# Routing the last tile by column halves, on rows that are not yet normalized

## The chip, the cores and the metric

The kernel runs on one core of one Trainium2 chip. The metric is the device time of one execution in microseconds (us): the median of several executions, 684.8 us for the kernel before. Below, PE or TensorE is the matrix engine, DVE or VectorE the vector engine, ACT or ScalarE the engine for activations, POOL or GpSimd the general engine, and SP the queue that issues the large loads. Each engine works through its own queue in order, and waits for others by semaphores.

## The reference, cut to what matters

One layer of a perceiver: cross-attention to a context of 1601 rows, a linear-attention block with an MLP, and a mixture of experts. There are 8 x 64 = 512 tokens of width 512. What the change touches is the end of the MLP, the layer norm after it and the routing:

```python
# end of the second block: x is (512, 512)
x = x + (gelu(h2 @ w1 + b1) @ w2 + b2) + ...
m = layernorm(x)                        # (x - mean) / sqrt(var + 1e-5)
router_logits = m @ w_router            # (512, 8)
top_w, top_i = jax.lax.top_k(router_logits, 2)
top_w = softmax(top_w)
for e in range(8):
    hmid = silu(m @ w0[e]) * (m @ w1[e])
    out = out + gating[:, e:e+1] * (hmid @ wo[e])
return x + out
```

## The kernel before, in words

All data are float32. The 512 tokens are four tiles (NT = 4) of 128 tokens, tokens on partitions; a row of 512 columns is KC = 4 chunks of 128. The order of the instructions on every engine is the order in which the program writes them out by hand. PSUM has eight banks: four in rotation for short products (`mm_bank`) and four for accumulators (`acc_bank`).

The MLP has 16 chunks of hidden columns. The first eight are multiplied by w2 for all four tiles at once; the last eight (HELD) are kept in SBUF and multiplied tile by tile (`last_chunks`), so that the routing of one tile can run beside the products of the next. `finish(t)` (lines 826 to 840) adds tile t's product to the residual row `xs`, takes its mean and variance with `bn_stats`, normalizes it into `mn`, and sends `mn` to a scratch in DRAM (`mn_dram`, on ACT's queue) and `xs` to the output (on GpSimd's). Then, while TensorE works on the chunks of tile t + 1:

- `turn_m` (L851, L853) transposes the four chunks of `mn` and ACT copies them to SBUF.
- `route` (L859 to L874) multiplies them by the router's columns, and DVE picks the two largest of the eight logits, their places, and marks them (`hot`, `member`).
- `rank_tile` (L888 to L894) counts by two small products how many earlier tokens have chosen each expert, and compares the rank with the numbers 1 to 128 (`slot`): a one-hot matrix for expert 0.
- `first_rows` (L899) multiplies `mn` by this one-hot: this gathers the first 128 rows of expert 0, already transposed, in one PSUM bank over all four tiles. These are called the gathering products.
- `tabulate` (L913 to L928) works out where each token stands in a table in DRAM and writes it with two indirect DMAs of GpSimd, each of which waits for the one before; `count_tile` keeps the running counts.

For the last tile there is no next tile; `turn_m`, `route`, `rank_tile` and `first_rows` follow each other. ACT copies the gathered rows (`xgT_first`, L959), DVE does the last two `tabulate`, a product sums the counts (L966), DVE copies them out (`count`, L968), and works out the gates (L971 to L981), which ACT writes to `mn_dram` (L982).

Then the experts run one after the other. `whole_tile` makes for each expert four products with the upper weights (`up`, L1081), silu and product (`gated`, L1044, L1046), transposes (`hidden_t`, L1052) and the lower product (`y`, L1089). The rows of the other experts are gathered from `mn_dram` by indirect DMAs (`fetch`, L1017), whose places come from the table (`late`, L984 and L1007 to L1011). The experts' weights pass through a ring of 12 tiles in SBUF, 1 MB each, that the SP queue refills (L192) as they are used up. The expert stage opens its own pool over the same eight PSUM banks, and its banks are placed in the order in which they are first named.

Of the kernel before, what the change touches and what calls it, by code (L numbers as in the profile page):

```python
# [20 lines left out]
P = 128  # L21
# [25 lines left out]
def perceiver_kernel(  # L47
# [189 lines left out]
    for e in range(NE):  # L237
# [18 lines left out]
        slot, pattern=[[1, P]], base=1, channel_multiplier=0, allow_small_or_imprecise_dtypes=True  # L256
    )
# [278 lines left out]

    for g in range(4):
        key_group(0, g)
    for g in range(2):
        key_group(1, g)  # L540
    for t in range(NT):
# [15 lines left out]
        if t == NT - 3:  # L557
            late_loads()

# [265 lines left out]

    def finish(t):
# [4 lines left out]
        mv = small.tile([P, 2], F32, tag="mv1", name=f"mv_m_{t}")  # L831
        nc.vector.bn_aggr(mv, st)
        rstd = small.tile([P, 1], F32, tag="rstd1", name=f"rstd_m_{t}")
        nc.scalar.activation(rstd, mv[:, 1:2], AF.Sqrt, bias=eps)
        nc.vector.reciprocal(rstd, rstd)
        nc.vector.tensor_scalar(
            mn[:, t, :D], xs[:, t, :], mv[:, 0:1], rstd, ALU.subtract, ALU.mult
        )
        nc.scalar.dma_start(mn_dram[t * P : (t + 1) * P, :D], mn[:, t, :D])
# [6 lines left out]
    m_ts = {}  # L846

    def turn_m(t):
        bank = mm_bank(f"tr_m_{t}")
        for c in range(KC):  # L850
            nc.tensor.transpose(bank[:, c * P : (c + 1) * P], mn[:, t, c * P : (c + 1) * P], ident)  # L851
        m_ts[t] = mlp2.tile([P, KC, P], F32, tag="mT", name=f"m_t_{t}")
        nc.scalar.copy(m_ts[t].rearrange("p c q -> p (c q)"), bank)  # L853

    def route(t):

        bank = mm_bank(f"router_{t}")
        for c in range(KC):
            nc.tensor.matmul(  # L859
                bank[:, :NE], m_ts[t][:, c, :], router[:, c, :], start=(c == 0), stop=(c == KC - 1)  # L860
            )
        logits = small.tile([P, NE], F32, tag="logits", name=f"logits_{t}")
        nc.vector.tensor_copy(logits, bank[:, :NE])
        nc.vector.max(out=top[:, t, :], in_=logits)
        where = small.tile([P, NE], mybir.dt.uint32, tag="where", name=f"where_{t}")
        nc.vector.max_index(out=where, in_max=top[:, t, :], in_values=logits)
        nc.vector.tensor_copy(chosen[:, t, :], where[:, :2])
# [3 lines left out]
            chosen[:, t, :, None].to_broadcast([P, 2, NE]),  # L871
# [4 lines left out]
    def count_tile(t):  # L876
        if t == 0:
            nc.vector.tensor_copy(members[:, 0, :], member[:, 0, :])
        else:
            nc.vector.tensor_tensor(members[:, t, :], members[:, t - 1, :], member[:, t, :], ALU.add)  # L880

    onehots = {}

    def rank_tile(t):

        bank = mm_bank(f"rank_{t}")
        if t > 0:
            nc.tensor.matmul(bank[:, :NE], ones, members[:, t - 1, :], start=True, stop=False)  # L888
        nc.tensor.matmul(bank[:, :NE], earlier, member[:, t, :], start=(t == 0), stop=True)
        nc.vector.scalar_tensor_tensor(  # L890
            rank[:, t, :], bank[:, :NE], 1.0, member[:, t, :], ALU.add, ALU.mult
        )
        onehots[t] = mlp2.tile([P, P], F32, tag="onehot", name=f"onehot_{t}")
        nc.vector.tensor_scalar(onehots[t], slot[:, :P], rank[:, t, 0:1], None, ALU.is_equal)  # L894

    def first_rows(t):

        for c in range(KC):
# [4 lines left out]
                start=(t == 0 and c == 0),  # L903
                stop=(t == NT - 1),
                skip_group_check=True,
            )

# [32 lines left out]
    for t in range(1, NT):  # L940

        last_chunks(t, range(0, 4))
        turn_m(t - 1)
        last_chunks(t, range(4, 5))
        route(t - 1)
        last_chunks(t, range(5, 7))
        rank_tile(t - 1)
        last_chunks(t, range(7, HELD))
        finish(t)
        first_rows(t - 1)  # L950
        if t > 1:
            tabulate(t - 2)
        count_tile(t - 1)
    turn_m(NT - 1)
    route(NT - 1)
    rank_tile(NT - 1)
    first_rows(NT - 1)
    xg_t0 = moe.tile([P, KC, P], F32, name="xgT_first")
    nc.scalar.copy(xg_t0.rearrange("p c q -> p (c q)"), first_bank)  # L959
# [452 lines left out]
```

## Time and profile before

| what | us |
|---|---|
| median of 3 runs | 684.8 (684.72 to 687.41) |
| the profiled execution's own time | 685.44 |
| its span | 683.7 |
| mean granted clock of TensorE | 0.983 of full speed |
| TensorE busy | 638.9 (93% of the span) |
| VectorE busy | 179.1 (26%) |
| ScalarE busy | 128.2 (19%) |
| GpSimd busy | 61.7 (9%) |

The span is counted from the first to the last event of one execution; the time of that execution has 1.7 us around it. Times in the text are from the start of the span. In the profile, PE stands for TensorE's products and PEld for its loading of weights; an entry such as `[2.01 <-DVE mn L836]` says that the engine stood idle for 2.01 us and that DVE's instruction of line 836 ended that. A float32 product over 512 columns appears as two records. The granted clock is 1.00 at full speed and 0.50 at half.

### The profile page before, as it was taken

What the parts mean: (1) busy time and instruction counts of PE and PEld (TensorE: products, weight loads), DVE (VectorE), ACT (ScalarE), POOL (GpSimd) and SP (SyncE); (2) the same over time, 40 slices, a digit from 0 to 9 for tenths busy, and PEclk for the clock granted to TensorE, in tenths of its full rate; (3) what the DMA queues carried; (4) which work ended last, traced back from release to release, by engine and by line L of the source; (5) the groups of instructions that cost most, each with busy time, mean ns of one, the idle gap of its engine ahead of it and who ended that gap; (6) DMA issues with size and microseconds to landing.
All of it is one profiled execution on the core that took longest, in us unless ns stands there. A gap on an engine that the chain in (4) does not pass through costs nothing. (4 is left out here: it accounts for less than half of the span.)

```text
span 683.7 us, 6217 instructions
## 1 busy us (share of the span) xinstructions
PE 638.9 (93%) x2376; PEld 296.2 (43%) x2376; DVE 179.1 (26%) x403; ACT 128.2 (19%) x240; POOL 61.7 (9%) x81
## 2 busy tenths in 40 slices
PE   4998989799999999999999998898999999989993
PEld 3643434244444444445444455543444344434441
DVE  4011323132228687670000035310311101110100
ACT  2241223220132121122011200211111111111110
POOL 2000000000000000041000002331012202120000
PEclk9999999999999999999999999699999999999998
DMA  8999999999601103021311323127397595694711
GB/s 328 418 420 385 418 385 413 370 367 422 232 13 62 62 0 124 1 69 55 112 62 73 106 79 126 61 61 265 136 390 257 199 357 175 233 348 175 283 17 18
DMA packets 24222, 138.04 MB, mean 202 GB/s; under 512 B 4164, under 2 KB 4164, under 8 KB 11896
## 3 DMA queue, kind: packets, MB, share of 16 engines
q1 hardware_dynamic: 20056, 129.90, 49.0%
q0 software_dynamic: 3024, 6.58, 4.3%
q10 hardware_dynamic: 1104, 1.07, 0.4%
q8 instruction: 23, 0.38, 0.2%
q14 instruction: 15, 0.12, 0.1%
HBM read 132.56 MB, written 4.97 MB: 201 GB/s over the span
## 5 line engine op out<-in xcount | busy, mean ns | idle before, releaser
L1081 PE MATMUL up<-e_up,xgT 128*128 128x512 f32 x224 | 100.2, 595 | 1.2 <-PEq L1310 1.2
L1081 PEld LDWEIGHTS up<-e_up,xgT 128*128 128x128 f32 x224 | 40.9, 190 | 50.4 <-issue 50.4
L1089 PE MATMUL y<-e_wo,hidT 128*128 128x512 f32 x128 | 61.0, 599 | 0.0
L792 PE MATMUL mlp<-w,hid_sb 128*128 128x512 f32 x128 | 58.8, 597 | 0.0
L1046 DVE TENSOR_TENSOR mid<-up,act 128x256 f32<-128x256 f32 x35 | 14.9, 425 | 164.2 <-ACT act L1044 159.7
L771 PE MATMUL hid<-v_sb,w 128*128 128x512 f32 (+2 forms) x144 | 56.6, 545 | 0.0
L472 PE MATMUL av<-ctx,eT 128*64 128x512 f32 x192 | 48.4, 617 | 7.3 <-DMA ctx<-in_ctx_dram 6.5
L423 PE MATMUL sc<-ctxT,pw_t 128*64 128x401 f32 (+1 forms) x256 | 48.1, 501 | 0.7 <-DMA ctxT<-in_ctx_T_dram 0.7
L771 PEld LDWEIGHTS hid<-v_sb,w 128*128 128x128 f32 x144 | 26.2, 190 | 29.1 <-issue 27.3
L792 PEld LDWEIGHTS mlp<-w,hid_sb 128*128 128x128 f32 x128 | 23.4, 190 | 24.9 <-issue 24.9
L1044 ACT ACTIVATE act<-up 128x256 f32<-128x256 f32 x35 | 13.4, 383 | 104.5 <-PE up L1081 95.7
L786 POOL TENSOR_TENSOR xin<-xin,b_bc 128x512 f32<-128x512 f32 x4 | 5.1, 1263 | 295.3 <-DVE rstd_h L728 291.1
L423 PEld LDWEIGHTS sc<-ctxT,pw_t 128*64 128x64 f32 x256 | 20.3, 136 | 26.3 <-issue 22.9
L1062 POOL DMA_INDIRECT out_dram<-y_sb,dst_late x11 | 16.8, 1529 | 161.1 <-ACTq L1310 103.7
L1089 PEld LDWEIGHTS y<-e_wo,hidT 128*128 128x128 f32 x128 | 22.4, 190 | 19.5 <-issue 19.1
L595 PE MATMUL wk<-h_t,wk 128*128 128x512 f32 x64 | 29.5, 604 | 0.0
L595 PE MATMUL wq<-h_t,wq 128*128 128x512 f32 x64 | 29.4, 602 | 0.0
L532 PE MATMUL v<-wv,h_t 128*128 128x512 f32 x64 | 28.7, 597 | 0.6 <-DVE h_t L519 0.6
L472 PEld LDWEIGHTS av<-ctx,eT 128*64 128x64 f32 x192 | 13.9, 140 | 35.3 <-issue 24.6
L691 PE MATMUL wo<-wo,a_t 128*128 128x512 f32 x64 | 28.6, 597 | 0.0
L671 DVE RECIPROCAL rden<-rden 128x512 f32<-128x512 f32 x8 | 26.8, 3354 | 0.3
L828 DVE TENSOR_TENSOR xs<-mlp,xs 128x512 f32<-128x512 f32 x4 | 2.8, 692 | 87.3 <-PE mlp L792 87.3
(230 smaller groups left out, 653.1 us busy)
## 6 DMA issues: line engine op xcount, KB each, us to landing
e_up<-in_L_ffn_up_dram SPq DMA_DIRECT2D x32, 1024.0 KB, 7.9
ctx<-in_ctx_dram SPq DMA_DIRECT2D x24, 1024.0 KB, 17.4
ctxT<-in_ctx_T_dram SPq DMA_DIRECT2D x24, 802.0 KB, 15.7
e_wo<-in_L_ffn_wo_dram SPq DMA_DIRECT2D x16, 1024.0 KB, 10.0
w<-in_L_attn_w_dram SPq DMA_DIRECT2D x8, 1024.0 KB, 11.7
ctxT<-in_ctx_T_dram SPq DMA_DIRECT2D x8, 796.0 KB, 16.7
big_up<-in_L_ffn_up_dram SPq DMA_DIRECT2D x4, 1024.0 KB, 7.9
wv<-in_L_attn_wv_dram SPq DMA_DIRECT2D x2, 1024.0 KB, 13.0
```

The source lines that it names most:

```text
L423: nc.tensor.matmul(sc[h * S : (h + 1) * S, :width], pw_t[:, c, (2 * t + h) * S : (2 * t + h + 1) * S], keys[h][:, c, :], start=(c == 0), s ...
L472: nc.tensor.matmul(av[h * S : (h + 1) * S, :], e_t[:, 4 * g + j, h * S : (h + 1) * S], rows[h][:, j, :], start=(g == 0 and j == 0), stop=F ...
L532: nc.tensor.matmul(bank, h_t[:, c, t * P : (t + 1) * P], wv_n[:, c, :], start=(c == 0), stop=(c == KC - 1))
L595: nc.tensor.matmul(bank, w[:, c, (j % 4) * P : (j % 4 + 1) * P], h_t[:, c, :], start=(c == 0), stop=(c == KC - 1),)
L671: nc.vector.reciprocal(rden, rden)
L691: nc.tensor.matmul(wo_banks[t], a_t[:, j, t * P : (t + 1) * P], wo_r[j // 4][:, j % 4, :], start=(j == 0), stop=(j == nj - 1),)
L771: nc.tensor.matmul(hid_banks[f][:, tokens], w[:, c, (f % 4) * P : (f % 4 + 1) * P], h2_t[:, c, tokens], start=(c == 0), stop=(c == KC - 1),)
L792: nc.tensor.matmul(acc[t], hid[:, t * P : (t + 1) * P], need("w2", f // 4)[:, f % 4, :], start=(f == 0), stop=(f == FF // P - 1),)
L1046: nc.vector.tensor_tensor(hid, bank[:, FQ:], act, ALU.mult)
L1062: nc.gpsimd.indirect_dma_start(out=out, out_offset=bass.IndirectOffsetOnAxis(ap=dst[:n, :], axis=0), in_=y_sb[:n, :], in_offset=None, boun ...
L1081: nc.tensor.matmul(bank, xg_t[:, c, :], up_of[q][:, c, :], start=(c == 0), stop=(c == KC - 1))
L1089: nc.tensor.matmul(y, h_t[:, j, :], w[:, 2 * (q % 2) + j, :], start=(q + j == 0), stop=(q + j == NQ))
```

## The change

The change rewrites the routing, above all that of the last tile.

- The router is centred: `centre_router`, called once in the attention stage, takes from each router column its mean over the 512 rows (`router_c`). The logits of rows that are not normalized then differ from those of normalized rows only by a factor for each row (one over the standard deviation), which does not change the order. So `turn_m` transposes `xs` in place of `mn`, and the difference of the two largest logits is multiplied by the factor (`rstds`) before the softmax.
- DVE reads the logits straight from PSUM, and the places of the two largest without a cast; two copies leave the chain. The one-hot is made from the rank's product directly, with `slot0` (0 to 127) and `member`.
- The last eight chunks of the last tile are multiplied by column halves: columns 0 to 255 first, then 256 to 511 into a bank of their own (`second_bank`). The first half is added, transposed and taken through the router while TensorE multiplies the second.
- The rows of the last tile are normalized by ACT, and no longer by DVE.
- The gathering products of tiles 0 to 2 leave the loop; they stand between the steps of the last tile's routing, four, two, five and one at a time, and those of tile 3 follow.
- The gathered rows are copied in two halves, by ACT and by DVE; `tabulate` for tiles 2 and 3 stands behind them on DVE. `tabulate` for tiles 0 and 1 comes one tile earlier. The sum of counts lies in a bank of the accumulators, and the expert stage names some of its banks first, so that they are placed elsewhere.

The core of the diff:

```diff
+    def centre_router():
+        bank = mm_bank("router_sums")
+        for c in range(KC):
+            nc.tensor.matmul(bank[:, :NE], ones, router[:, c, :], start=(c == 0), stop=(c == KC - 1))
+        nc.vector.scalar_tensor_tensor(
+            router_c, bank[:, None, :NE].to_broadcast([P, KC, NE]), -1.0 / D, router, ALU.mult, ALU.add,
+        )
...
             late_loads()
+            centre_router()
...
-    def turn_m(t):
+    def turn_m(t, chunks=range(KC)):
...
-            nc.tensor.transpose(bank[:, c * P : (c + 1) * P], mn[:, t, c * P : (c + 1) * P], ident)
+            nc.tensor.transpose(bank[:, i * P : (i + 1) * P], xs[:, t, c * P : (c + 1) * P], ident)
...
-        logits = small.tile([P, NE], F32, tag="logits", name=f"logits_{t}")
-        nc.vector.tensor_copy(logits, bank[:, :NE])
+        logits = route_banks[t][:, :NE]
         nc.vector.max(out=top[:, t, :], in_=logits)
...
-        nc.vector.tensor_scalar(onehots[t], slot[:, :P], rank[:, t, 0:1], None, ALU.is_equal)
+        nc.vector.tensor_scalar(
+            onehots[t], slot0, bank[:, 0:1], member[:, t, 0:1], ALU.is_equal, ALU.mult
+        )
...
+    st = small.tile([P, 2, 6], F32, tag="st2", name="st_m_last")
+    half_chunks(0, range(0, 5))
+    turn_m(t - 1)
+    rank_before(t - 1)
+    half_chunks(0, range(5, HELD))
+    for h in range(2):
+        nc.vector.tensor_tensor(xs[:, t, halves[h]], acc[t][:, halves[h]], xs[:, t, halves[h]], ALU.add)
+    logits_of(t - 1)
+    choose(t - 1)
+    half_chunks(1, range(0, 3))
+    turn_m(t, range(0, 2))
+    nc.vector.bn_stats(st[:, 0, :], xs[:, t, halves[0]])
+    half_chunks(1, range(3, 5))
+    rank_tile(t - 1)
+    count_tile(t - 1)
+    half_chunks(1, range(5, 7))
+    logits_of(t, range(0, 2))
+    rank_before(t)
+    half_chunks(1, range(7, HELD))
+    nc.vector.tensor_tensor(xs[:, t, halves[1]], second_bank[:, :HD], xs[:, t, halves[1]], ALU.add)
+    first_rows(4)
+    turn_m(t, range(2, KC))
+    nc.vector.bn_stats(st[:, 1, :], xs[:, t, halves[1]])
+    mv, rstd = moments(t, st)
+    nc.vector.scalar_tensor_tensor(neg_mean, mv[:, 0:1], -1.0, rstd, ALU.mult, ALU.mult)
+    nc.scalar.activation(mn[:, t, :D], xs[:, t, :], AF.Identity, bias=neg_mean, scale=rstd)
+    first_rows(2)
+    logits_of(t, range(2, KC))
+    choose(t)
+    first_rows(5)
+    rank_tile(t)
+    first_rows(1)
+    count_tile(t)
+    first_rows(KC)
+
+    bank = acc_bank("counts")
+    nc.tensor.matmul(bank[:, :NE], ones, members[:, NT - 1, :], start=True, stop=True)
+    xg_t0 = [moe.tile([P, 2, P], F32, name=f"xgT_first_{h}") for h in range(2)]
+    for h, copy in enumerate([nc.scalar.copy, nc.vector.tensor_copy]):
+        copy(xg_t0[h].rearrange("p c q -> p (c q)"), first_bank[:, halves[h]])
+    write(NT - 1)
     for t in range(NT - 2, NT):
         tabulate(t)
-
-    bank = mm_bank("counts")
-    nc.tensor.matmul(bank[:, :NE], ones, members[:, NT - 1, :], start=True, stop=True)
     count = moe.tile([P, NE], F32, name="count")
     nc.vector.tensor_copy(count, bank[:, :NE])
...
     nc.vector.tensor_tensor(e2, top[:, :, 1], top[:, :, 0], ALU.subtract)
+    nc.vector.tensor_tensor(e2, e2, rstds, ALU.mult)
...
+        for tag, n in (("mm1", 2), ("y1", 1), ("yw", 1)):
+            pse.tile([P, 512], F32, tag=tag, bufs=n, name=f"place_{tag}")
```

## The prediction

> **What bounds the kernel now.** I read the page first, then the timeline around the step between the MLP and the experts, then busy time by stretches cut to the steps of the clock, then what GpSimd waits for. The page:
>
> ```profile
> span 683.7 us, 6217 instructions
> PE 638.9 (93%) x2376; PEld 296.2 (43%) x2376; DVE 179.1 (26%) x403; ACT 128.2 (19%) x240; POOL 61.7 (9%) x81
> ...
> PE   4998989799999999999999998898999999989993
> ...
> PEclk9999999999999999999999999699999999999998
> ```
>
> TensorE is busy 93% of the span, so time comes only from its few holes. The clock row has one low slice, the 26th (427 to 444 us), inside what the change touches: the end of the MLP and the routing of the last tile. The timeline there:
>
> ```profile
> 424.15 1.05 PE L899 MATMUL first_rows<-onehot,mn 128*128 128x128 f32 x8
> ...
> 424.42 0.69 DVE L828 TENSOR_TENSOR xs<-mlp,xs 128x512 f32<-128x512 f32 x1 [0.54 <-PE mlp L792]
> ...
> 427.22 0.66 PE L851 MATMUL tr_m<-ident,mn 128*128 128x128 f32 x4 [2.01 <-DVE mn L836]
> ...
> 428.60 1.88 PE L859 MATMUL router<-col,m_t 128*128 128x8 f32 x8 [0.73 <-ACT m_t L853]
> ...
> 431.83 0.60 PE L889 MATMUL rank<-member,earlier 128*128 128x8 f32 x2 [0.92 <-DVE member L874]
> ...
> 435.64 0.16 DVE L968 COPY count<-counts 128x8 f32<-128x8 f32 x1
> ...
> 435.91 9.98 PE L1081 MATMUL up<-e_up,xgT_first 128*128 128x512 f32 x16 [0.60 <-ACT xgT_first L959]
> ```
>
> The last tile's chain (add, statistics, normalize, transpose, router, choice, rank, gather) is serial: TensorE waits 2.0, 0.7, 0.9, 0.6 and 0.6 us in it, and from the end of the MLP (424.3) to the first expert product (435.91) pass 11.6 us. The products also run cold: the router's take 1.88 us here and 1.04 for earlier tiles, and the 16 records of `up` take 9.98 us where 16 take 6.84 at full clock. The stretches of 3.41 us show the rule of the clock:
>
> ```profile
> 59.41:62.83 3.42, 1.13 (x5) 0.34 (x6) 1.82 (x1) 1.53 (x2) 0.00 (x0) 1.00 1.02 307
> 62.83:66.24 3.41, 3.41 (x11) 0.97 (x8) 0.00 (x0) 0.28 (x2) 0.00 (x0) 0.50 1.00 412
> ...
> 127.68:131.09 3.41, 1.51 (x8) 0.63 (x10) 0.00 (x0) 1.60 (x2) 0.00 (x0) 1.00 1.00 291
> 424.64:428.06 3.42, 1.22 (x10) 0.79 (x8) 2.82 (x14) 0.39 (x2) 1.82 (x2) 1.00 0.75 266
> 428.06:431.47 3.41, 2.30 (x10) 2.21 (x10) 1.20 (x9) 0.49 (x1) 0.99 (x1) 0.50 0.52 205
> ...
> 434.88:438.30 3.42, 2.82 (x6) 1.51 (x6) 1.82 (x14) 2.07 (x3) 0.97 (x1) 0.50 0.01 0
> 438.30:441.71 3.41, 3.41 (x5) 1.35 (x4) 0.41 (x3) 0.00 (x0) 1.38 (x2) 0.50 0.08 5
> ```
>
> The first number after the length is PE busy, the third from the end the granted clock. The clock falls at 428.06 and returns at 441.71, exactly four steps of 3.413 us. On this grid a stretch with 1.13 or 1.22 us of work is followed by half clock, one with 1.51 is not; cold stretches with 2.30 to 2.82 us of work stay cold, only a full one (3.41) ends it. `up` starts at 435.91 and loses half of 441.71 - 435.91, that is 2.9 us. The table writes:
>
> ```profile
> 436.01 0.97 POOL L928 DMA_INDIRECT table<-named,spot  x1 [2.37 <-DVE e L971]
> ...
> 443.68 0.97 POOL L928 DMA_INDIRECT table<-named,spot  x1 [1.41 <-DMA table<-named,spot]
> 446.09 0.59 POOL L984 DMA_DIRECT2D late<-table  x1 [1.45 <-DMA table<-named,spot]
> 451.51 1.06 POOL L1017 DMA_INDIRECT xg<-mn_dram,src_late  x1 [4.83 <-PE ht L1052]
> ```
>
> each waits for the one before (about 2.4 us a piece), and the second expert's rows hang on them.
>
> **The change, part by part.** I rebuild TensorE's queue from the order of the changed program, with zero at the first chunk of tile 3. In the trace that is 415.37. The gathering products of tiles 0 and 1 (1.05 us each, L899) leave the loop, which has no other wait of TensorE, so zero moves to 413.3.
>
> Prices at full clock: a chunk over 512 columns 0.855 us; over 256 columns two records of 0.219 (48 records of `pw` in 10.53 us), so 16 halves cost 7.0 where 8 wholes cost 6.84: 0.2 us more, added at the end. Four transposes 0.43, a router over four chunks 0.9, one small rank product 0.26, a gathering product 0.26. DVE: add or copy of 128x256 0.42 (row of `mid`), half a bn_stats 0.35 (half of 0.69), small operations 0.2 apart. ACT copy of 128x256 0.37 (row of `hidT`).
>
> The queue then is: half 0 with the transposes and carried rank of tile 2 until 4.1; router of tile 2 5.0; half 1 interleaved with two transposes of tile 3, rank of tile 2, half a router and the carried rank until 9.6 (members of tile 2 are ready at 8.6, needed at 8.9). DVE adds half 1 by 10.1, while TensorE makes four gathering products (10.65) and the last two transposes (10.9). ACT copies until 11.35; two gathering products fill that; router 11.85. ACT's square root stands behind this copy, so reciprocal and negated mean are done at 12.1, and hold the choice 0.2 us. The choice without its two copies is 0.85 us (max, index, hot, member, 0.2 each and 0.09): 12.95; five gathering products cover it until 13.15. Rank 13.45, one-hot 13.8, four gathering products 14.9, counts 15.2. From the end of the MLP to the last gather the old chain took 10.7 us (424.3 to 435.0); here it takes 5.3 (9.6 to 14.9), all but some 0.5 of it filled with products.
>
> Unknown forms: max and index straight from PSUM (a DVE copy from PSUM is 0.17, like one from SBUF; bounds 0 to 0.1 each; I take 0), two per-row operands in the one-hot (0.29 to 0.41; 0.29 as the old row), ACT's Identity of 512 (0.58 as its copy; covered by 1.1 us of gathering products, exposed it would cost what is over). All together between -0.2 and +0.6.
>
> **Where the stall goes.** ACT copies half the first rows (15.0 to 15.35), DVE the other half (15.8; it waits for ACT). Rows alone would let `up` start near 15.4. But in the changed program the first `up` also waits on DVE for `count` (L1070), since its PSUM bank held `counts`; the old one has that wait too (435.80, beside the copy's 435.70, so it cost nothing). Old DVE ran both `tabulate` calls while TensorE gathered, from 432.94 on; the new one has them behind the half copy, bare: 2.7 us from 432.94 to 435.64, then 0.16. So `up` starts at 15.8 + 2.9 = 18.7, with the 0.2 of the halves 18.9, in the trace's time 413.3 + 18.9 = 432.2. TensorE stands still about 3.5 us there.
>
> Start to start 435.9 - 432.2 is 3.7; the old cold loss of 2.9 also goes: 6.6 less what the new wait costs in clock. This is where a rule must be weighed. Rows: a stretch holding 2.2 to 2.3 us of idleness lost the clock twice, one with 1.9 did not. A hole of 3.5 us leaves 2.0 or more on one side of a boundary in about 85 of 100 positions. The Trainium skill (TensorE: Matmul & The Clock Gate, Part 1) says the gate falls after at least one idle window of 3.4 us and that the windows run free. By the rule a hole of 3.5 must meet a boundary almost exactly, the clock survives, and the sum is 6.6. By the rows it is usually lost: with the boundary early in the hole `up` has one cold stretch (1.7 us, about 44 in 100), with it late a partial one and a full one (1.6 to 3.3, mostly 2.8; 41 in 100). I follow the rows: 6.6 - 1.7 = 4.9 at the commonest, 6.6 - 2.8 = 3.8 next. The profiled execution took 685.44 (span 683.7 and 1.7 around it): 680.5 or 681.6. It is 0.6 above the median of 684.8, so against that the gain reads 4.3; I use the absolute figure, since the old loss also moves with the boundaries.
>
> **What hides the rest.** `router_sums` (four products, 0.9 us) and `router_c` stand in the attention stage, ahead of waits of 0.8 and 2.7 us of TensorE for `ctx`; uncovered, 0.9. `slot0` is a GpSimd iota of 0.24 at 3 us, while its queue has nothing due. SP: the load behind the first half of w2 goes out 1.3 us later (419.0 to 420.3), the other 1.2 earlier; both are for expert 1, needed at 470: cover 40 us. ACT: the write of the last `mn` now stands behind the row copy (428.7); the gathers reading it start after 440; its 0.3 us of issue precede an Exp that waits for DVE until 432.5. Late next: the gating write must land before ACT's first Silu, since its buffer is reused: 432.1 + 1.8 + 2.2 = about 436.1, Silu's table load, the Silu and the product done by 438.2 against TensorE's 439.0: 0.8 us to spare. GpSimd: tile 1's table entries and the `out` write go earlier; the four last writes run from 430.9, `late` is read at about 440.5 (5.6 earlier), while TensorE's own steps come 3.8 to 6.6 earlier. In the old run the gathers had 2.6 us to spare at 459, and `late` lay landed 1.6 us before DVE took it. No wait.
>
> **Rivals.** First, the clock survives the hole (the rule, or a lucky boundary): 678.8, chance 0.14. Second, the table chain slips: a write held 2.9 instead of 2.4 us (one is, at 441.30), four of them 2 us and the gathers land late; 1 to 3 us of the gain return: 681.5 to 683.5, chance 0.05. Third, the engines' small steps, not TensorE's filler, set the tail: three uncovered hand-overs as in the old chain (2.0, 0.7, 0.9) bring 3 us back and 684 results: 0.04. Fourth, slower: the tail is all narrow products (256, 128 and 8 columns); if the gate counts these as too little work the clock falls before the hole. Each us of the 13 us of tail work then costs another, and the re-warming takes 3.4: with more than 3.2 us of it cold, the 6.6 are gone; from the start of half 1 some 8 us are cold, about 690. Against it: the same narrow products between 396 and 424 keep the clock at 1.00. Chance 0.03.
>
> **How the numbers follow.** Likeliest, 0.74: clock lost, 680.5 to 681.6; I say 680.5. Range 677.6 (clock kept, small forms cheap) to 683.0 (two cold stretches, the unknown forms at +0.6, part of the slipped table chain). 0.5%, about what a measurement of this kernel can tell from no change, is 3.4 us: faster below 681.4. The first case gives 0.64 of faster and 0.10 of same, the kept clock 0.14 of faster, slipped tables 0.05 and small steps 0.04 of same, the cold tail 0.03 of slower: 0.78, 0.19, 0.03.
>
> **What would show it.** Right: TensorE without a wait over 0.5 us from the loop to `counts`; then one of 3 to 3.5 us before `up`, ended by DVE's `count`, with two `tabulate` calls on DVE inside it; half clock for one or two stretches after; `up` at about 432; `late` near 440. Wrong: `up` released by the ACT or DVE row copy; clock at 1.00 throughout; waits in the choice or rank of tile 3; a wait of TensorE for `xg` or of `ht` for `mid` in expert 0.

## The result and the profile after

The changed kernel takes 680.08 us (median of 6 runs, 677.87 to 681.70) against 684.98 (6 runs, 684.72 to 687.41) of the kernel before: ratio 0.9917, 95% interval 0.9901 to 0.9934. The forecast was 680.5 us, with a range of 677.6 to 683.0. The profiled execution after took 679.42 us, with a span of 677.7 and a mean granted clock of 0.989. The page after:

```profile
span 677.7 us, 6271 instructions
PE 635.5 (94%) x2400; PEld 297.5 (44%) x2400; DVE 178.9 (26%) x405; ACT 128.8 (19%) x242; POOL 61.7 (9%) x82
...
PE   4998999899999999999999999798999899999993
...
PEclk9999999899999999999999999899999999999997
```

The 26th slice of the clock row, 6 before, is 8. The 8th is 8 as well: one stretch of 3.41 us at half clock, called a cold stretch below, in the attention stage (at 127.2 us), which the change hardly touches. The kernel before has one there too, at 62.8 us; the two slices, which print as 8 and 9, lie on either side of a rounding. The timeline between the MLP and the second expert:

```profile
424.57 1.36 PE L953 MATMUL first_rows<-onehot,mn 128*128 128x128 f32 x10
425.77 0.29 PE L937 MATMUL rank<-member,earlier 128*128 128x8 f32 x2
...
426.59 1.13 PE L953 MATMUL first_rows<-onehot,mn 128*128 128x128 f32 x8 [0.21 <-DVE onehot L939]
427.56 0.29 PE L1061 MATMUL counts<-members,ones 128*128 128x8 f32 x2
427.76 0.37 ACT L1064 COPY xgT_first<-first_rows 128x256 f32<-128x256 f32 x1 [2.21 <-PE first_rows L953]
428.16 0.43 DVE L1064 COPY xgT_first<-first_rows 128x256 f32<-128x256 f32 x1 [1.50 <-ACT xgT_first L1064]
...
429.65 0.16 DVE L979 SCALAR_TENSOR_TENSOR spot<-over,at 128x2 uint32<-128x2 f32 x1
...
430.89 0.16 DVE L979 SCALAR_TENSOR_TENSOR spot<-over,at 128x2 uint32<-128x2 f32 x1
430.97 0.16 DVE L1070 COPY count<-counts 128x8 f32<-128x8 f32 x1
431.23 8.68 PE L1188 MATMUL up<-e_up,xgT_first 128*128 128x512 f32 x16 [3.39 <-issue]
...
438.26 0.42 DVE L1153 TENSOR_TENSOR mid<-up,act 128x256 f32<-128x256 f32 x1 [4.79 <-ACT act L1151]
439.75 0.38 PE L1159 MATMUL ht<-ident,mid 128*128 128x128 f32 x2
440.30 0.60 POOL L1087 DMA_DIRECT2D late<-table  x1 [1.44 <-DMA table<-named,spot]
```

TensorE has no wait over 0.21 us from the loop to `counts`. Then it stands still for 3.39 us: the rows are ready when DVE's half copy ends at 428.59, but `up` starts only behind the copy of `count` at 430.97, and the two calls of `tabulate`, each of which ends with a `spot`, lie between. The profile names no releaser here (`issue`); that it is `count` is what the first experiment asks. The transposes of the first expert (`ht`) do not wait for `mid`.

Busy time by stretches cut to the steps of the clock (PE's busy time comes first after the length, the granted clock is the third number from the end), in the attention stage and at the change:

```profile
123.79:127.20 3.41, 1.06 (x4) 0.21 (x4) 1.82 (x1) 2.81 (x3) 0.00 (x0) 1.00 1.07 310
127.20:130.61 3.41, 3.41 (x8) 0.99 (x10) 0.00 (x0) 0.42 (x2) 0.00 (x0) 0.50 0.96 357
...
424.17:427.59 3.42, 3.21 (x28) 3.05 (x28) 1.65 (x11) 0.89 (x2) 0.39 (x1) 1.00 0.92 346
427.59:431.00 3.41, 0.25 (x4) 0.16 (x2) 2.50 (x22) 1.66 (x2) 0.91 (x1) 1.00 0.28 107
431.00:434.41 3.41, 3.18 (x4) 1.51 (x5) 1.99 (x13) 0.21 (x1) 1.06 (x2) 0.50 0.09 5
434.41:437.83 3.42, 3.42 (x9) 1.52 (x8) 0.00 (x0) 1.28 (x1) 0.97 (x1) 1.00 0.01 0
```

At the change the clock is lost for one stretch (431.00 to 434.41), where before it was lost for four. One cold stretch of full work costs about 1.7 us, half its length.

### The profile page after: what moved, and what is told of

It reads as the page before. It is cut to its first block, busy times and chain, and to the rows that moved or that the text cites. A ratio compares the mean times of both kernels' runs of the same rounds, so it can differ in the third digit from the quotient of the medians.

```text
span 677.7 us, 6271 instructions
## 1 busy us (share of the span) xinstructions
PE 635.5 (94%) x2400; PEld 297.5 (44%) x2400; DVE 178.9 (26%) x405; ACT 128.8 (19%) x242; POOL 61.7 (9%) x82
## 5 line engine op out<-in xcount | busy, mean ns | idle before, releaser
L1153 DVE TENSOR_TENSOR mid<-up,act 128x256 f32<-128x256 f32 x35 | 14.9, 424 | 163.5 <-ACT act L1151 159.0
L814 PE MATMUL mlp<-w,hid_sb 128*128 128x512 f32 x112 | 51.0, 597 | 0.0
L814 PEld LDWEIGHTS mlp<-w,hid_sb 128*128 128x128 f32 x112 | 20.7, 190 | 23.5 <-issue 23.4
```

Of the source, the lines that this page charges most:

```text
L814: nc.tensor.matmul(acc[t], hid[:, t * P : (t + 1) * P], need("w2", f // 4)[:, f % 4, :], start=(f == 0), stop=(f == FF // P - 1),)
L1153: nc.vector.tensor_tensor(hid, bank[:, FQ:], act, ALU.mult)
```

## A measure that leaves the attention stage out

The times of these versions carry cold stretches of the attention stage that come and go. To set them apart I read two places in each profiled execution: DVE's add of tile 0 (the first `xs<-mlp,xs` of the MLP's end, called the add below) and the first `up`. What lies behind the add is what the change can touch; where the add itself stands is the attention stage's affair.

| kernel | add stands at | add to `up` | `up` to the end | add to the end | median of the times |
|---|---|---|---|---|---|
| before | 396.62 | 39.29 | 247.79 | 287.08 | 684.98 |
| after | 395.90 | 35.33 | 246.47 | 281.80 | 680.08 |
| count_first | 396.13 | 32.86 | 246.01 | 278.87 | 677.01 |
| no_place | 396.43 | 35.33 | 246.64 | 281.97 | 679.98 |
| fill_hole | 394.37 | 35.48 | 244.85 | 280.33 | 676.57 |
| fill_narrow | 394.69 | 35.49 | 246.72 | 282.21 | 681.44 |
| centre_only | 395.99 | 39.05 | 247.86 | 286.91 | 683.90 |
| centre_chain | 394.48 | 35.94 | 248.18 | 284.12 | 680.33 |
| rows_in_loop | 396.16 | 37.96 | 246.98 | 284.94 | 683.19 |
| whole_tile_last | 394.11 | 35.44 | 246.65 | 282.09 | 679.95 |
| early_gates | 394.30 | 32.55 | 245.15 | 277.70 | 673.90 |
| early_gates_again | 396.49 | 32.55 | 245.16 | 277.71 | 675.84 |
| early_whole | 396.01 | 34.59 | 245.00 | 279.59 | 677.32 |
| early_whole_late_table | 396.23 | 32.62 | 244.95 | 277.57 | 677.12 |

Each row is one execution, and its end is read to 0.1 us, so the two columns that run to the end are good to about 0.05 us. The add stands near 394.3 where no cold stretch lies ahead of it, and 1.6 to 2.2 us later with one from about 127 on (in after at 127.2). An early one need not cost this: fill_narrow has one at 61.6 and its add at 394.69, while in before, with one at 62.8, the add stands at 396.62. In before the last rows of the context also come later (TensorE goes on at 129.58, in fill_narrow at 127.66); why is open. By this measure the change is worth 287.08 - 281.80 = 5.28 us: 3.96 ahead of `up`, and 1.32 behind it, which is what the clock accounts for: half of 441.71 - 435.91 before, half of 434.41 - 431.23 after. The two profiled spans differ by 6.0, since their attention stages differ by 0.72 as well.

## The experiments

**count_first: the wait for `count` alone.** The copy of `count` goes ahead of the two calls of `tabulate`.

```diff
+    count = moe.tile([P, NE], F32, name="count")
+    nc.vector.tensor_copy(count, bank[:, :NE])
     for t in range(NT - 2, NT):
         tabulate(t)
-
-    count = moe.tile([P, NE], F32, name="count")
-    nc.vector.tensor_copy(count, bank[:, :NE])
```

> The changed kernel with one edit: the copy of `count` stands ahead of the two last `tabulate` calls on VectorE. My theory (the 3.4 us hole before `up` is the wait for `count`, which stands behind 2.5 us of table work): `up` starts at about 428.8 in place of 431.2, the hole shrinks to about 1.0 us and the clock stays at 1.00. Not all of it arrives: the gates still come at the same time, their write lands near 435.0, Silu's table load and the product end near 437.1, so the first `ht` waits about 1.5 us and comes at 437.1 in place of 439.75. Gain over the changed kernel 2.6 us in the profile, median about 677.5. Rival one (rows and copies set the start of `up`, and `count` only comes at the same time): no change, 680. Rival two (nothing is late behind it): 4.0 to 4.6 us, 675.5 to 676.

677.01 us (5 runs, 675.69 to 678.58), ratio to before 0.989 (0.987 to 0.991). Its timeline:

```profile
428.99 7.11 PE L1187 MATMUL up<-e_up,xgT_first 128*128 128x512 f32 x16 [0.92 <-ACT xgT_first L1064]
...
434.82 1.28 ACT L1150 ACT_TABLE_LOAD   x1 [2.95 <-DMA mn_dram<-mn]
...
437.01 0.44 PE L1158 MATMUL ht<-ident,mid 128*128 128x128 f32 x2 [0.92 <-DVE mid L1152]
```

The wait before `up` falls from 3.39 to 0.92, so what held `up` was the place of the copy of `count`; DVE now ends its half of the rows and `count` at 428.89, and `up` follows at 428.99. The 16 records take 7.11 us, the clock held. But DVE gives the gates no earlier than before, so their write lands late, ACT's table load for the first silu waits for it, and `ht` waits 0.92 us for `mid`. A moved wait uncovers the next one, with its own price.

**no_place: is it the bank?** The expert stage's banks are no longer named first.

```diff
-        for tag, n in (("mm1", 2), ("y1", 1), ("yw", 1)):
-            pse.tile([P, 512], F32, tag=tag, bufs=n, name=f"place_{tag}")
```

> The changed kernel without the lines that name some banks of the expert stage first (place_mm1, place_y1, place_yw). The prediction said that `up` waits for `count` because its bank held the counts. If that is the cause, another placing takes the wait away: `up` near 428.6, and about 2.6 us less, 677.5. The rival: the expert stage opens a new pool over all eight banks, and its first product waits for every last reader of the old pool, wherever its own bank lies; the program's order still lists VectorE up to `count` ahead of `up`. Then `up` stays at 431.2, the hole at 3.4 us, and the median at 680. I now hold the rival for likelier.

679.98 us (4 runs), ratio 0.9922 (0.9902 to 0.9943); from add to `up` 35.33 us, as in the full change to the hundredth. In its timeline the same wait stands before `up`:

```profile
431.76 4.81 PE L1186 MATMUL up<-e_up,xgT_first 128*128 128x512 f32 x7 [3.38 <-issue]
```

So the wait does not come from the bank that `counts` lay in. In the built program `counts` lies in bank 6 and the first `up` in bank 4, or in bank 0 where the naming is left out: they never shared one. With either placing `up` waits on DVE for the position of `count`; that opening the new pool makes its first product wait for the last readers of the whole old pool is how I read this, and it was not tried in another way. The naming of banks brings nothing here that these executions show (0.17 us by the traces).

**fill_hole and fill_narrow: what the clock counts.** Twelve products that nobody reads stand between `counts` and `up`; over 128 columns in the one, over 8 in the other.

```diff
+    spare_bank = mm_bank("filler")
+    for i in range(12):
+        nc.tensor.matmul(
+            spare_bank[:, :P], mn[:, i // KC, (i % KC) * P : (i % KC + 1) * P], onehots[i // KC], start=True, stop=True
+        )
```

(fill_narrow has `[:, :NE]` at the bank and at the one-hot, NE being 8.)

> The changed kernel with 12 products of 128 columns added behind the counts, into a bank that nobody reads: about 3.1 us of work in the hole, nothing else moved. Theory of the clock (a stretch of 3.41 us with 2 us or more of idleness is followed by half clock): the clock stays at 1.00 in every execution, `up` starts at the same time (431.2), and the median falls by the mean cold loss, about 2 us, to 678; the spread of 677.9 to 681.7 narrows to about 0.5 us. Rival (the loss in the first `up` has another cause, or the spread comes from elsewhere): 680 as before, with the same spread. If the added products run past the copy of `count`, `up` starts later by that.

> This is fill_hole with the twelve extra products over 8 columns in place of 128; nobody reads them. They fill the wait for count with records of TensorE just as before (about 3.1 us busy), but nearly all of that is loading of weights. Reason to ask: in early_whole a stretch of 3.41 us with 2.69 us of busy records, half of them transposes and 8-column router products, lost the clock, and in centre_chain one with 1.76 and in rows_in_loop one with 1.99; in count_first one with 2.50, mostly 512-column products, kept it. Theory (the gate counts the columns that stream, not the time of records): the clock falls for one or two stretches after the filler although TensorE looks busy through it, up x16 takes 8 to 10 us, and the time is that of the full change, 678.5 to 681. Rival (the gate counts busy records): clock at 1.00 from 424 to 440, up x16 at 7.1, and the time of fill_hole, 676.4 to 678.9.

fill_hole took 676.57 us (5 runs, 676.40 to 678.89), ratio 0.9892 (0.9873 to 0.9911); fill_narrow 681.44 (5 runs, 678.62 to 681.56), ratio 0.9934 (0.992 to 0.9947). In fill_hole's timeline:

```profile
426.17 2.92 PE L1064 MATMUL filler<-onehot,mn 128*128 128x128 f32 x24
...
429.85 7.10 PE L1193 MATMUL up<-e_up,xgT_first 128*128 128x512 f32 x16 [0.76 <-DVE e L1078]
```

and in fill_narrow's, from `up` after the same filler, the same wait and the same place behind the add:

```profile
426.49 2.83 PE L1064 MATMUL filler<-onehot,mn 128*128 128x8 f32 x24
...
430.18 8.80 PE L1193 MATMUL up<-e_up,xgT_first 128*128 128x512 f32 x16 [0.87 <-DVE e L1078]
```

fill_narrow cut to the steps of its clock:

```profile
426.79:430.20 3.41, 2.54 (x24) 2.48 (x23) 2.86 (x24) 1.41 (x2) 1.00 (x1) 1.00 0.20 79
430.20:433.61 3.41, 3.41 (x4) 1.44 (x5) 1.62 (x9) 0.21 (x1) 0.97 (x1) 0.50 0.09 5
```

fill_hole has 1.00 throughout this step; its stretch over the same filler is

```profile
425.91:429.33 3.42, 3.18 (x29) 2.99 (x27) 2.38 (x20) 1.66 (x2) 0.77 (x1) 1.00 0.30 115
```

The two fillers keep TensorE busy for nearly the same time (2.92 and 2.83 us), and one kernel keeps the clock where the other loses it: a record over 8 columns is nearly all loading of weights (2.48 us of PEld beside 2.54 of PE), and does not hold the clock. The other executions agree: the mean granted clock of the five of fill_hole is 0.990 to 0.995, of fill_narrow 0.985 to 0.990. From add to `up` they are equal with the full change (35.48, 35.49 and 35.33), so fill_hole's gain at the change is the clock alone: 246.47 - 244.85 = 1.62 us behind `up`, against the 1.6 of one cold stretch. The rest of the 3.0 us between the two profiled executions is the attention stage (394.37 against 395.90). The times still spread over 2.5 us (3.8 in the full change), where I had expected 0.5, so the hole is not the only cause of the spread.

**centre_only and centre_chain: the centred router without the rest.** Both keep the old loop, with the last tile whole and the gathering products of each tile in the loop; what they take from the change is the centred router, the logits straight from PSUM and the one-hot made in one step. In centre_only `count_tile` stands behind `tabulate` on DVE and the last write ahead of ACT's copies; in centre_chain `count_tile` goes ahead of it and the write behind the last row copy (the diff of centre_chain to centre_only, cut):

```diff
         rank_tile(t - 1)
+        count_tile(t - 1)
         last_chunks(t, range(7, HELD))
         finish(t)
         first_rows(KC)
-        if t > 1:
-            tabulate(t - 2)
-        count_tile(t - 1)
+        if t < NT - 1:
+            tabulate(t - 1)
...
     nc.scalar.copy(xg_t0.rearrange("p c q -> p (c q)"), first_bank)
+    write(NT - 1)
```

> The kernel before with one part of the change: the centred router, transposes of rows not yet normalized, logits from PSUM without the two copies. No column halves, gathering products and `tabulate` where they were. My working: the transposes of the last tile follow its last gathering product of tile 2 at once (2.0 us of wait gone), copy 0.6, router 0.9 at full clock, the choice behind VectorE's normalizing at about 3.0 us after the add, rank, one-hot, gathering product; VectorE then does both `tabulate` calls during the gathering products, so that `count` is ready about 2 us after the rows and `up` starts near 431.5 to 432, no later than in the changed kernel, with a hole of 2 us. So nearly the whole gain from this part alone: 678.5 with the clock kept, 680 to 681.5 with it lost, median about 680. Rival (halves and gathering products between the steps carry the gain): under half of it, 682.5 to 683.5.

> The centring alone once more. The first try had two waits of its own: TensorE's carried rank product stood ahead of the router and waited 2.9 us for `members`, and ACT's copy stood behind the issue of the write of `mn`. Here `count_tile` follows the rank at once, and the write of the last `mn` follows the copy of the rows. Working: transposes at 1.0 us after the last chunk, copy 0.6, router 0.9, choice held by VectorE's normalizing for 0.1, then 0.85, rank 0.3, one-hot 0.4, rows 1.05; `count` behind both `tabulate` calls 2 us after the rows. `up` then starts as in the changed kernel, within 0.5 us, and the median is 679.5 to 681, by how often the clock is lost. Rival (gathering products between the steps and halves are needed): 682.5 or more.

centre_only took 683.90 us (22 runs), ratio 0.9983 (0.9973 to 0.9994), worse than theory and rival had it. TensorE's timeline there has a wait that my own order had made: the carried rank, the product that counts the choices of earlier tiles, waits for `members`, which DVE computed behind `tabulate`:

```profile
427.84 0.57 PE L932 MATMUL rank<-members,ones 128*128 128x8 f32 x2 [2.87 <-DVE members L922]
```

centre_chain, with that mended, took 680.33 (6 runs), ratio 0.9923 (0.9907 to 0.994): in time the same as the full change. By the traces it is 284.12 - 281.80 = 2.3 us short of it behind the add, 0.6 of it ahead of `up` and 1.7 behind, in the clock. Its stretches:

```profile
422.89:426.30 3.41, 1.76 (x14) 1.57 (x14) 2.07 (x8) 0.77 (x2) 0.72 (x2) 1.00 0.92 310
426.30:429.71 3.41, 2.70 (x12) 2.61 (x12) 2.41 (x24) 0.00 (x0) 0.43 (x1) 0.50 0.21 80
```

Three stretches run cold (to 436.54). So by these traces more than half of what the full change gains over the old kernel, 2.96 of 5.28 us, comes from the centred router with its shorter chain; by the medians, 680.33 and 680.08, all but 0.3 us. What the ordering around it is worth shows only once the wait for `count` is gone (early_gates, below).

**rows_in_loop and whole_tile_last: the fillers and the halves.** In rows_in_loop the gathering products of tiles 0 to 2 go back to the loop and to the place behind the MLP (first diff); in whole_tile_last the last tile is multiplied, added, transposed and routed over 512 columns, with the fillers kept (second diff, its end).

```diff
         last_chunks(t, range(7, HELD))
         finish(t)
+        first_rows(KC)
...
-    first_rows(2)
-    first_rows(5)
-    first_rows(1)
```

```diff
-    half_chunks(1, range(5, 7))
-    logits_of(t, range(0, 2))
-    rank_before(t)
-    half_chunks(1, range(7, HELD))
-    nc.vector.tensor_tensor(xs[:, t, halves[1]], second_bank[:, :HD], xs[:, t, halves[1]], ALU.add)
+    last_chunks(t, range(7, HELD))
+    nc.vector.tensor_tensor(xs[:, t, :], acc[t], xs[:, t, :], ALU.add)
     first_rows(4)
-    turn_m(t, range(2, KC))
-    nc.vector.bn_stats(st[:, 1, :], xs[:, t, halves[1]])
+    turn_m(t)
+    rank_before(t)
+    nc.vector.bn_stats(st[:, 0, :], xs[:, t, :])
```

> The changed kernel with the gathering products of tiles 0 and 1 back in the loop; those of tile 2 stay behind the last half chunk, nothing stands between the later steps. The loop gets 2.1 us longer, the tail waits at the router (0.4), the choice (1.1) and the one-hot (0.4) but is only 0.25 us shorter: `up` 1.85 us later, 681.9 median, and about 2.5 with a clock lost more often. Rival (the filler only fills, and the hole before `up` takes up the difference): 680.

> The changed kernel with the last tile multiplied over all 512 columns, as the other tiles, and the gathering products between its steps kept. Without halves two transposes (0.22), half a router (0.45) and the carried rank (0.26) move behind the last chunk, while the gathering products fill the waits as before: the router ends 0.2 to 0.3 us later, the 0.2 us that the halves cost is saved. Expected within 0.5 us of the changed kernel, 679.8 to 680.5. Rival (the halves carry a good part of the gain, since the longer add, statistics and copy, 0.27, 0.27 and 0.21 us, come bare into the chain): 681 or more.

rows_in_loop took 683.19 us (9 runs), ratio 0.9959 (0.9943 to 0.9974). The waits in TensorE's timeline are back, 0.46, 0.96 and 0.54 us, with 3.29 before `up`, and the clock is lost from 428.48 on: 284.94 - 281.80 = 3.1 us worse behind the add, and 3.1 by the medians. The fillers, as I call the gathering products between the steps, are worth that. whole_tile_last took 679.95 (6 runs), ratio 0.9919 (0.9901 to 0.9938), the same as the full change, and 282.09 behind the add: while the wait for `count` stands, the halves bring 0.3 us at most.

**early_gates: the version that the experiments point to.** DVE's work of the tail is put in the order of need. `tabulate` of tile 2 goes right behind its counts; the gates are worked out ahead of the row copy; then one copy of the rows, the copy of `count`, and the last `tabulate`.

```diff
     rank_tile(t - 1)
     count_tile(t - 1)
+    tabulate(t - 1)
...
-    xg_t0 = [moe.tile([P, 2, P], F32, name=f"xgT_first_{h}") for h in range(2)]
-    for h, copy in enumerate([nc.scalar.copy, nc.vector.tensor_copy]):
-        copy(xg_t0[h].rearrange("p c q -> p (c q)"), first_bank[:, halves[h]])
-    write(NT - 1)
-    for t in range(NT - 2, NT):
-        tabulate(t)
-    count = moe.tile([P, NE], F32, name="count")
-    nc.vector.tensor_copy(count, bank[:, :NE])
     e2 = moe.tile([P, NT], F32, name="e2")
...
     nc.vector.tensor_tensor(gating, gating, hot2g, ALU.add)
+    xg_t0 = moe.tile([P, KC, P], F32, name="xgT_first")
+    nc.scalar.copy(xg_t0.rearrange("p c q -> p (c q)"), first_bank)
+    write(NT - 1)
+    count = moe.tile([P, NE], F32, name="count")
+    nc.vector.tensor_copy(count, bank[:, :NE])
+    tabulate(NT - 1)
```

> The changed kernel with VectorE's queue set in order of need: `tabulate` of tile 2 in the hole of VectorE behind `count_tile` of tile 2; the gates (e2 to gating, with ACT's Exp) ahead of the copies of the rows; one row copy by ACT in place of two halves in series; then `count`, then `tabulate` of tile 3. Theory (what stood ahead of `count` and of the gates on VectorE is the whole of what remained): `up` about 0.9 us after the last gathering product, hole 0.6 us, clock kept; the gates' write leaves 4 us earlier, so Silu is ready before the second `up` ends and no `ht` waits; `late` about 5 us earlier. Against the changed kernel 2.8 us of hole and about 2 of clock: 675.3 to 676 median; against the run with only `count` moved (677.0) 1.5 better. Rival (the gates' write or GpSimd's chain is late all the same): no better than 677. Rival two (VectorE now delays the rows' one-hot): worse than 677.

> The kernel of early_gates, unchanged, a second time. Reason: from tile 0's add to the end early_whole_late_table takes 277.57 us and early_gates 277.70, so by the traces they are equal, yet their times are 677.1 and 673.9; the whole difference lies ahead of the change, where tile 0's add stands at 394.30 in early_gates and at 396.23 in early_whole_late_table, after a cold stretch of the clock at 127 us. Theory (that stretch falls by chance in executions of any version, and the five runs of early_gates were lucky): this time some runs show granted clocks of 0.986 to 0.99 and times of 675.5 to 677.7, median 674 to 677, and from tile 0's add to the end of the profiled execution still 277.5 to 278. Rival (the halves, or the place of tabulate, spare the stage ahead of them the stretch): again 673.7 to 674.2 in all runs with clocks of 0.992 to 0.995.

673.90 us the first time (5 runs, 673.69 to 674.15), ratio 0.9829 (0.9813 to 0.9845); 675.84 the second (4 runs, 675.29 to 675.96), ratio 0.9857 (0.9836 to 0.9877). Both beat the kernel before and the full change; the first beat its own forecast, 675.3 to 676, too. The timeline of the first:

```profile
426.16 0.59 ACT L1078 COPY xgT_first<-first_rows 128x512 f32<-128x512 f32 x1 [0.55 <-PE first_rows L953]
...
426.59 0.16 DVE L1081 COPY count<-counts 128x8 f32<-128x8 f32 x1
...
426.85 7.11 PE L1187 MATMUL up<-e_up,xgT_first 128*128 128x512 f32 x16 [0.61 <-ACT xgT_first L1078]
...
433.79 0.38 PE L1158 MATMUL ht<-ident,mid 128*128 128x128 f32 x2
...
435.15 0.60 POOL L1086 DMA_DIRECT2D late<-table  x1 [1.44 <-DMA table<-named,spot]
```

`count` is copied while ACT still copies the rows, the clock holds, nothing waits behind. The two profiled executions agree behind the add (277.70 and 277.71); they differ by the attention stage alone (394.30 and 396.49), and so do their times. The two sets ran on different chips, but there the kernel before took 685.33 and 685.17, so the chip is no explanation. So the interval of one set of runs understates the uncertainty: it holds for the executions that were drawn. Of the 4.10 us that early_gates gains behind the add over the full change, moving `count` alone (count_first) brings 2.93; the single row copy and the earlier gates were not tried apart.

**early_whole and early_whole_late_table: the halves once more, with the wait for `count` gone.** The first is early_gates with the last tile whole; the second also moves `tabulate` of tile 2 behind the copy of `count`.

```diff
     count_tile(t - 1)
-    tabulate(t - 1)
     last_chunks(t, range(7, HELD))
...
-    tabulate(NT - 1)
+    for t in range(NT - 2, NT):
+        tabulate(t)
```

> This is early_gates with the column halves of the last tile undone: its last eight chunks are multiplied over 512 columns, added and transposed whole; the gathering products between the steps, the early gates and the early tabulate stay. Theory (the gathering products cover the last tile's steps, and the halves add nothing to that): the same time as early_gates, 673.4 to 674.4 us, with first up product within 0.3 us of early_gates' place after the first chunk of tile 3, and the clock at 1.00 through the step. Rival (the halves matter, but the 3.4 us wait for count hid it in whole_tile_last, because TensorE only arrived earlier or later at a wait that DVE ended): without the halves TensorE waits in the tail for the add, the transposes' copy or the choice, 0.5 to 1.5 us together, and up starts that much later: 674.5 to 675.5 us, or 676 and more where these waits cost the clock as well.

> This is early_whole with the tabulate of tile 2 moved on DVE from ahead of the last tile's add to behind the copy of count, in front of that of tile 3. In early_whole it held the add back, and TensorE's transposes waited 0.66 us for it. Theory (that placing, and not the missing halves, cost early_whole its 3.4 us against early_gates): no wait of TensorE over 0.3 us before counts, the clock stays at 1.00 through the step, late near 437 and no wait behind it, 673.5 to 675 us. Rival (the halves are what covers the last tile's steps): waits of 0.5 us and more for the add, the copy or the choice remain, and 676 to 678 us.

early_whole took 677.32 us (5 runs, 676.15 to 678.77), ratio 0.9877 (0.986 to 0.9894). The theory's 673.4 to 674.4 failed. `tabulate` held up the last tile's add on DVE, and TensorE's transposes waited 0.66 us; then the clock fell. Cut to its steps:

```profile
422.16:425.57 3.41, 2.69 (x23) 2.32 (x22) 2.11 (x7) 1.24 (x3) 0.97 (x1) 1.00 0.87 288
425.57:428.98 3.41, 3.41 (x17) 3.24 (x17) 1.56 (x11) 1.64 (x3) 0.96 (x1) 0.50 0.07 24
```

A stretch with only 0.72 us of idleness lost the clock; 2.01 us of its work were transposes, the router and a rank, mostly loading of weights. That is what fill_narrow was then made to test. early_whole_late_table took 677.12 (4 runs, 675.55 to 677.73), ratio 0.9877 (0.9862 to 0.9892). Here my number of 673.5 to 675 failed and its reason held: no wait in the tail, the clock at 1.00, 277.57 us behind the add against 277.70 of early_gates. The time is longer by its attention stage (the add at 396.23, a cold stretch from 127.8). So where the clock holds, the last tile needs no halves: the fillers cover its steps. Whether it keeps the clock as often is open. Two of the four executions took 677.7 us at a mean clock of 0.986, which none of the nine of early_gates shows (0.990 at the least), and where they lost it was not profiled. Nor do the medians, 677.32 and 677.12, tell early_whole from early_whole_late_table: what `tabulate` costs is read from one execution of each.

## Why the prediction was right, and where it was not

**Total.** The likeliest case came true: 680.5 forecast, 680.08 measured. The working was 3.7 us by the earlier start of `up` and 1.2 by the clock (2.9 cold before, 1.7 after), 4.9 together. Behind the add the traces show 3.96 and 1.32, 5.28 together. The other 0.7 us between the two profiled spans was not in the working at all; that the median came within 0.4 us of the forecast is in part luck, since the forecast started from one execution and the six after it spread over 3.8 us.

**TensorE's queue.** Tile 3's first chunk was put at 413.3 and is at 412.70; the attention stage, 0.72 us shorter in this execution, accounts for that, so the step is right to 0.1. `counts` was put at 15.2 behind it and stands at 14.9; `up` at 18.9 and stands at 18.5. The fillers cover what they were said to cover: rows_in_loop lacks them and shows the waits.

**The new wait.** Forecast 3.5 us behind two `tabulate` calls, measured 3.39. Right in place, size and releaser (count_first), wrong in reason: I put it down to the bank that held `counts`, and no_place shows the same wait with other placing.

**The clock in the hole.** I followed the rows against the rule of the Trainium skill (TensorE: Matmul & The Clock Gate, Part 1: at least one idle window of 3.4 us) and forecast one cold stretch as the commonest. One came, 431.00 to 434.41, behind a stretch with 0.25 us of work; with 44 chances in 100 against 41 for a longer loss, that it was just one is luck. A stretch need not be idle to lose the clock, so the rule as I read it is too narrow. But my form of it, a bound on idleness between 1.9 and 2.3 us, is wrong as well. centre_chain lost the clock with 1.65 us of idleness in a stretch, fill_narrow with 0.87, early_whole with 0.72. (In rows_in_loop it is 1.88: the 1.99 us of work that I named for it comes from stretches cut 0.5 us off the steps of its clock.) Where all products are wide the bound did hold, with a narrower gap. In the attention stages of the fourteen traces, from 16 us on, where nearly all work is products over 398 to 512 columns, every stretch with 1.41 us of work or less was followed by half clock, and none with 1.51 or more, the figure that the prediction showed. The largest that lost it is centre_only's:

```profile
58.73:62.15 3.42, 1.41 (x7) 0.48 (x8) 1.82 (x1) 1.53 (x2) 0.00 (x0) 1.00 1.00 307
```

What fits all of them is to add up the time in which columns stream. A worked example, an estimate from rows (a product over 512 columns takes 0.855 us, so one over 128 streams 0.21): in early_whole's stretch the four transposes stream 0.43, the gathering products some 0.7, router and rank under 0.1, so 1.2 of 3.41 us, below that 1.41, though TensorE looks busy for 2.69. In the full change the stretch 424.17 to 427.59 has ten gathering products, by the same count 2.1 us, and kept the clock. No run tells whether the transposes count like the others. The prediction also has it that only a full stretch ends the cold: here one with 3.18 us of work did.

**The rivals.** The kept clock did not come in the profiled execution. Tables and gathers: `late` forecast at 440.5, read at 440.30, and TensorE waits for no gathered rows (`xgt` at 452.6). Small steps: only 0.21 us. The fourth rival, slower because the gate counts narrow products as too little, had a true mechanism and a wrong reach. fill_narrow shows it; but in the changed kernel the gathering products over 128 columns stand between the narrow ones, and the stretch named above kept the clock. My evidence against it, that narrow products between 396 and 424 keep the clock, was weak: there they stand among 512-column products.

**Unknown forms.** The one-hot took 0.35 us (I took 0.29, bounds to 0.41), ACT's normalization 0.81 (I took 0.58; covered as said), the half of bn_stats 0.42 (0.35), the choice straight from PSUM 0.17 an operation as taken. Together they did not show: `counts` came 0.3 us earlier than forecast.

**The gates.** Forecast 0.8 us to spare; `mid` is done at 438.68 and `ht` runs at 439.75, about 1 us. count_first, which brings `up` forward by 2.5 us (counted from the add), turns just this into a wait of 0.92.

**What I left out** is the cause of the spread. I saw it in the hole at the change; it is at least as much in the attention stage.

## What to carry to other kernels

When a chain on one engine is shortened, list what the other engines still have queued ahead of the first instruction of the next stage, and put that in the order of need: here another order at the end of the tail, mostly DVE's, was worth 4.1 us, beside the 5.3 of the change itself. Fill holes of TensorE with products that stream many columns; loading weights for 8 columns fills the timeline and not the clock. Compare versions from a common event behind the noisy stage, and not by the end time alone.

## What the hardware did that I had not expected

The clock falls with TensorE busy 2.54 or 2.69 of 3.41 us, where the records are narrow (fill_narrow, early_whole), and holds with 2.50 where they are `up` products over 512 columns, as count_first shows:

```profile
435.58:438.99 3.41, 2.50 (x8) 1.04 (x7) 1.18 (x3) 1.18 (x3) 1.84 (x2) 1.00 0.01 0
```

The same holes of the attention stage cost nothing or 1.7 us, by where the stretches of the clock fall. TensorE waits for `ctx` in after and in early_gates, 2.32 and 2.45 us:

```profile
127.18 4.91 PE L477 MATMUL av<-ctx,eT 128*64 128x512 f32 x13 [2.32 <-DMA ctx<-in_ctx_dram]
```

```profile
127.26 3.22 PE L477 MATMUL av<-ctx,eT 128*64 128x512 f32 x13 [2.45 <-DMA ctx<-in_ctx_dram]
```

The shorter wait was followed by half clock, the longer one by full. In after nearly the whole hole lies in one stretch, the one with 1.06 us of work above; in early_gates a step falls at 125.53, inside the wait, and each side has work enough:

```profile
122.12:125.53 3.41, 2.21 (x10) 0.47 (x6) 1.54 (x1) 1.88 (x2) 0.00 (x0) 1.00 1.03 359
125.53:128.95 3.42, 1.69 (x8) 0.63 (x10) 0.28 (x1) 1.72 (x2) 0.00 (x0) 1.00 1.00 288
```

Where the steps fall differs from execution to execution of one kernel (early_gates has no cold stretch in its first profile and one from 129.03 in its second), and here it moves a run by up to 2.2 us, where the change under study is worth 5.3.
